# Six instead of seven key tiles added on VectorE, and layer-norm statistics by bn_stats, in a two-layer graph attention kernel

## The chip, the cores and the metric

The kernel runs on one core of a Trainium2 chip. The metric is the device time of one execution in microseconds, lower is better. Before the change it is 4522.25 us, the median of three runs (4520.34 to 4522.34).

## What is computed

There are 8 entries of 2048 nodes with 256 features, and one adjacency matrix of 2048 x 2048 for all. Each entry goes through two attention layers, each with a residual and a layer norm behind it:

```python
def _layernorm(x, axis=-1, eps=1e-5):
    m = jnp.mean(x, axis=axis, keepdims=True)
    v = jnp.var(x, axis=axis, keepdims=True)
    return (x - m) / jnp.sqrt(v + eps)

# layer 0, 8 heads of 32 features
x_proj = jnp.einsum('bnd,hdf->bhnf', x, W)
e = leaky_relu(e_src[..., :, None] + e_dst[..., None, :], 0.2)
e = e + (softplus(beta_tilde) * jnp.log(prior + 1e-6))[:, None, :, :]     # prior = adj
attn = softmax(where(adj > 0, e, neg_inf), axis=-1)
h = jnp.einsum('bhij,bhjf->bhif', attn, x_proj)      # ... reshaped to (B, N, D)
x = _layernorm(x + h @ W_out.T)

# layer 1, one head of 256 features
e = leaky_relu(jnp.einsum('bnd,bmd->bnm', x @ W1, x @ W2), 0.2)
attention = softmax(where(adj > 0, e, -1e12), axis=-1)
x = _layernorm(x + relu(jnp.einsum('bnm,bmd->bnd', attention, x @ W3)))
```

The softmax of layer 0 needs, for each query and head, the sum over 2048 keys of the unnormalised weights, the denominator. The layer norm needs a mean and a variance of each row of 256.

## The kernel before

Layer 0 goes over 4 head pairs x 16 key tiles = 64 steps per entry. A step makes one product `s` of 128 keys x 2048 queries per head on VectorE, and TensorE multiplies `s` by the values (`val`) and by the denominators' weights (`den`):

```python
SUMMED = (1, 3, 5, 7, 9, 11, 13)
...
mt = self.mts[jt] if first else load_mt(jt)
s = []
for a in range(HP):                                            # HP = 2 heads
    h = hp * HP + a
    sa = wide_tile("s", "s", 4)
    nc.vector.scalar_tensor_tensor(sa, self.cs[a], self.re[:, 0, jt, h:h + 1], mt, ALU.max, ALU.mult)
    s.append(sa)
...
summed = self.b > 0 and jt in SUMMED
if self.b > 0 and jt - 1 in SUMMED[1:]:
    for d, sa, h in zip(self.sums, self.last, heads):
        nc.vector.scalar_tensor_tensor(d, sa, e[:, jt - 1, h:h + 1], d, ALU.mult, ALU.add)   # line 311
self.last = s
self.products(self.val, [v[:, jt, ts(h, DH)] for h in heads], s, jt == 0, jt == NT - 1)
if self.b > 0 and jt == SUMMED[0]:
    self.sums = [wide_tile("d", "d", 2) for _ in heads]
    for d, sa, h in zip(self.sums, s, heads):
        nc.scalar.activation(d, sa, AF.Copy, scale=e[:, jt, h:h + 1])
if not summed:
    self.products(self.den, [e[:, jt, h:h + 1].to_broadcast([P, DH]) for h in heads], s, jt == 0,
                  self.b == 0 and jt == NT - 1)
if self.b > 0 and jt == NT - 1:
    self.products(self.den, [ones] * HP, self.sums, False, True)
```

For a key tile in `SUMMED` the denominator's share is not multiplied on TensorE: the tile is scaled and added into `d`, one tile per head, and `d` is multiplied by ones once at the end of the head pair. The first of them is scaled by ScalarE, the rest are added by VectorE one step later. Entry 0 has no such sums.

`products` issues eight matmuls, four of 32 columns beside one another in the array (two heads, two halves of the queries); each fp32 matmul shows as two records in the trace.

The residual and the norm, used in `output` on each of 16 row tiles after the W_out product `y` (which lies in one of three PSUM slots), and at the end of each of the 16 layer-1 steps of an entry:

```python
def add_norm(z, a, b):
    f = small.tile([P, 6], F32, name="f", bufs=3)
    total, shift, squares, log, factor, bias = (f[:, k:k + 1] for k in range(6))
    nc.vector.tensor_tensor_reduce(z, a, b, 1.0, 0.0, ALU.add, ALU.add, total)
    nc.scalar.mul(shift, total, -1.0 / D)
    sq = small.tile([P, D], BF16, name="sq", bufs=1)
    nc.scalar.activation(sq, z, AF.Square, bias=shift, accum_out=squares)
    nc.scalar.activation(log, squares, AF.Ln, bias=eps_ln, scale=1.0 / D)
    nc.scalar.activation(factor, log, AF.Exp, scale=-0.5)
    nc.scalar.activation(bias, factor, AF.Identity, scale=shift)
    nc.scalar.activation(z, z, AF.Identity, bias=bias, scale=factor)
```

Layer 1 of one entry and layer 0 of the next run woven together. The order of TensorE is that of the program; the other engines are ordered by the scheduler:

```python
if dot is not None:
    dot.step()                                     # the last layer-1 step of the entry before
layer_0(2)                                         # two steps ahead of the W_out products
for k, _ in enumerate(gat.output()):               # 16 W_out products with their norm
    if k % 8 == 7:
        layer_0(1)
for k, _ in enumerate(gat.turn()):                 # 16 transposes and h3 products
    if k % 2 == 1:
        layer_0(1)
dot = Dot(gat)
dot.step(lambda k: layer_0((2, 1, 1)[k]))
for i in range(NT - 2):
    dot.step(lambda k: layer_0((0, 2 - (i % 2 == 1), 2 - (i % 14 == 13))[k]))
```

The stretch from the W_out products to the end of `turn` is called the seam here, the layer-1 steps after it the long stage. A seam and a long stage make a cycle; there are seven cycles with layer-0 work of a next entry, and an eighth without.

Of the kernel before, what the change touches and what calls it, by code (L numbers as in the profile page):

```python
# [9 lines left out]
F32 = mybir.dt.float32  # L10
BF16 = mybir.dt.bfloat16
I32 = mybir.dt.int32
AF = mybir.ActivationFunctionType
ALU = mybir.AluOpType
# [4 lines left out]
P = 128  # L19
# [8 lines left out]
def kernel(  # L28
# [26 lines left out]
    nc = tc.nc  # L55
    B, N, D = x.shape
# [6 lines left out]
    HP = 2  # L63
    NP = H // HP
    IG = BK // P
    SUMMED = (1, 3, 5, 7, 9, 11, 13)

    const = ctx.enter_context(tc.tile_pool(name="const", bufs=1))
    dram = ctx.enter_context(tc.tile_pool(name="dram", bufs=1, space=DRAM))
# [3 lines left out]
    small = ctx.enter_context(tc.tile_pool(name="small", bufs=3))  # L73
# [3 lines left out]
    def mm_tile(name):  # L77
        return ps.tile([P, BK], F32, tag="mm", name=name)

    def wide_tile(name, tag, bufs, dtype=F32):  # L80
        return wide.tile([P, N], dtype, tag=tag, name=name, bufs=bufs)
# [12 lines left out]
    eps_ln = const.tile([P, 1], F32)  # L94
# [92 lines left out]
        nc.vector.tensor_scalar(pen, a, 0.0, NO_EDGE, ALU.is_le, ALU.mult)  # L187
        nc.sync.dma_start(pen_d[ts(it, P), :], pen)

    def add_norm(z, a, b):  # L190

        f = small.tile([P, 6], F32, name="f", bufs=3)
        total, shift, squares, log, factor, bias = (f[:, k:k + 1] for k in range(6))
        nc.vector.tensor_tensor_reduce(z, a, b, 1.0, 0.0, ALU.add, ALU.add, total)  # L194
        nc.scalar.mul(shift, total, -1.0 / D)
        sq = small.tile([P, D], BF16, name="sq", bufs=1)
        nc.scalar.activation(sq, z, AF.Square, bias=shift, accum_out=squares)  # L197
        nc.scalar.activation(log, squares, AF.Ln, bias=eps_ln, scale=1.0 / D)
        nc.scalar.activation(factor, log, AF.Exp, scale=-0.5)
        nc.scalar.activation(bias, factor, AF.Identity, scale=shift)  # L200
        nc.scalar.activation(z, z, AF.Identity, bias=bias, scale=factor)  # L201

    def row_tile(name, bufs=4):
        return small.tile([P, D], F32, tag="row", name=name, bufs=bufs)


    class Gat:
# [80 lines left out]
        def step(self, count=1):  # L288

            for _ in range(count):  # L290
                hp, jt = next(self.units)
                if jt == 0:
                    self.cs = [self.query_rows(hp * HP + a) for a in range(HP)]
                    self.val = pacc.tile([P, HALF], F32, tag="val", name="val")
                    self.den = pacc.tile([P, HALF], F32, tag="den", name="den")
                first = self.b == 0 and hp == 0
                while first and len(self.mts) < min(jt + 2, NT):
                    self.mts.append(make_mt(len(self.mts)))
                mt = self.mts[jt] if first else load_mt(jt)
                s = []  # L300
                for a in range(HP):
# [4 lines that stand above are left out]
                v, e = self.v, self.re[:, 1]  # L306
                heads = [hp * HP + a for a in range(HP)]
# [3 lines that stand above are left out]
                        nc.vector.scalar_tensor_tensor(d, sa, e[:, jt - 1, h:h + 1], d, ALU.mult, ALU.add)  # L311
# [11 lines that stand above are left out]
                if jt == NT - 1:  # L323
                    self.finish(hp)
# [33 lines left out]
        def output(self):  # L358


            b = self.b
            self.h3 = h3 = whole.tile([P, NT, D], F32, tag="h3", name="h3")
            xb = x[b].rearrange("(t p) d -> p t d", p=P)
            for g in range(NB):
                nc.sync.dma_start(h3[:, ts(g, IG), :], xb[:, ts(g, IG), :])
            for it in range(NT):
                y = mm_tile("y")
                for g, ht in enumerate(self.hts):
                    nc.tensor.matmul(y[:, 0:D], ht[:, ts(it, P)], wot[:, g, :], start=(g == 0), stop=(g == 1))  # L369
                z = h3[:, it, :]  # L370
                add_norm(z, y[:, 0:D], z)
                nc.sync.dma_start(x1_d[b, ts(it, P), :], z)
                yield

# [19 lines left out]
    class Dot:  # L394
# [33 lines left out]
        def step(self, fill=lambda k: None):  # L428


            it, (p, den) = self.at, self.ahead
            self.at += 1
            fill(0)

            def turned(g):
                t = mm_tile("pt")
                for k in range(IG):
                    nc.tensor.transpose(t[:, ts(k, P)], p[:, ts(g * IG + k, P)], ident)  # L438
                pt = chunk.tile([P, BK], F32, tag="pt", name="pts", bufs=2)
                nc.scalar.copy(pt, t)  # L440
                return pt

            pt = turned(0)
            if it + 1 < NT:
                if (it + 1) % IG == 0:
                    self.queries((it + 1) // IG)
                self.scores(it + 1)
            fill(1)
            acc = pacc.tile([P, D], F32, tag="acc", name="acc")
            for g in range(NB):  # L450
                now, pt = pt, turned(g + 1) if g + 1 < NB else None
                for k in range(IG):
                    j = g * IG + k
                    nc.tensor.matmul(acc, now[:, ts(k, P)], self.h3[:, j, :], start=(j == 0), stop=(j == NT - 1))  # L454
            fill(2)
            rec = small.tile([P, 1], F32, name="rec1", bufs=2)
            nc.vector.reciprocal(rec, den)
            xr = row_tile("x1r")
            nc.sync.dma_start(xr, x1_d[self.b, ts(it, P), :])
            z = row_tile("z")  # L460
            nc.scalar.activation(z, acc, AF.Relu, scale=rec)  # L461
            add_norm(z, z, xr)
            nc.sync.dma_start(out[self.b, ts(it, P), :], z)


# [70 lines left out]
```

## Time and profile before

| | before |
|---|---|
| time, median of 3 runs | 4522.25 us |
| span of the profiled execution | 4520.6 us |
| first W_out product (end of entry 0's layer 0) | 579.4 us |
| one cycle of an entry, from W_out product to W_out product | 510.6 to 518.2 us |
| last cycle, without layer-0 work | 328.3 us |
| granted TensorE clock, mean | 0.980 |

In the profile a group of instructions has one row: line, engine, operation, output and inputs by their names in the program, shapes and count, then the busy time and the mean duration of one, then the idle time of the engine just before them and the engine that ended it. A row of waits names who waited, for whom, how long in total, how often, and the longest. Durations of instructions that follow one another on an engine overlap a little, so the price of one in a queue is read from start to start.

### The profile page before, as it was taken

The page shows a single profiled execution, that of the slowest core. Times are in us where ns is not written, and L with a number is a line of the kernel's source. Part 1 is how long each engine was busy: PE and PEld are TensorE (multiplying, and loading weights), DVE is VectorE, ACT ScalarE, POOL GpSimd, SP SyncE. Part 2 cuts the span into 40 slices and gives each one's busy share as a digit, 9 for nine tenths or more (in the row PEclk, how much of TensorE's full clock was granted, in tenths as well). Part 3 has the DMA queues.
Part 4 walks back from the last instruction along what each step waited for, and adds up shares of the span by engine and source line. Part 5 has one row for each costly group of instructions (what it writes and reads, how often), then busy time and mean ns, then how long its engine had stood idle before and what let it go on. Part 6 is the DMA issues. An engine that isn't in the chain of part 4 may idle for free. (4 is left out here: it accounts for less than half of the span.)

```text
span 4520.6 us, 60051 instructions
## 1 busy us (share of the span) xinstructions
PE 4247.3 (94%) x24476; PEld 2206.4 (49%) x24476; DVE 3651.3 (81%) x2397; ACT 1930.6 (43%) x4251; POOL 4.5 (0%) x14
## 2 busy tenths in 40 slices
PE   6888889999999989999999999999899999999899
PEld 4433334445454544455444554455454554455566
DVE  5787798888989988898998988898988989898111
ACT  6622244345343454344433453344443453443555
POOL 0000000000000000000000000000000000000000
PEclk9999999999999999999999999999999999999999
DMA  7788865556555465556554565555555565554211
GB/s 218 260 297 320 313 207 181 182 184 220 179 178 178 171 217 179 184 187 207 194 178 169 182 218 184 178 187 195 195 175 181 185 222 178 182 177 141 68 49 40
DMA packets 252773, 851.97 MB, mean 188 GB/s; under 512 B 33616, under 2 KB 152400, under 8 KB 174928
## 3 DMA queue, kind: packets, MB, share of 16 engines
q1 hardware_dynamic: 252496, 848.13, 54.1%
q8 instruction: 192, 3.15, 0.3%
q14 instruction: 85, 0.70, 0.0%
HBM read 772.15 MB, written 75.37 MB: 187 GB/s over the span
## 5 line engine op out<-in xcount | busy, mean ns | idle before, releaser
L304 DVE SCALAR_TENSOR_TENSOR s<-c,re,mt 128x2048 f32<-128x2048 f32 x1024 | 2352.4, 2348 | 179.7 <-PE den L329 70.9
L329 PE MATMUL val<-s,v 128*32 128x512 f32 x8192 | 1054.8, 612 | 128.8 <-DVE s L304 118.9
L454 PE MATMUL acc<-h,pts 128*128 128x256 f32 x4096 | 953.6, 381 | 22.0 <-ACT pts L440 22.0
L419 PE MATMUL e<-x1t,h 128*128 128x512 f32 x2048 | 904.1, 594 | 0.1
L454 PEld LDWEIGHTS acc<-h,pts 128*128 128x128 f32 x4096 | 748.0, 190 | 119.3 <-ACT pts L440 30.8
L311 DVE SCALAR_TENSOR_TENSOR d<-s,re,d 128x2048 f32<-128x2048 f32 x336 | 782.7, 2347 | 0.0
L329 PE MATMUL den<-s,re 128*32 128x512 f32 x5056 | 642.9, 599 | 0.0
L329 PEld LDWEIGHTS val<-s,v 128*32 128x32 f32 x8192 | 245.3, 111 | 758.4 <-issue 494.6
L419 PEld LDWEIGHTS e<-x1t,h 128*128 128x128 f32 x2048 | 379.4, 190 | 450.3 <-issue 423.7
L421 ACT ACTIVATE p<-e 128x512 f32<-128x512 f32 x512 | 303.6, 596 | 479.7 <-PE e L419 479.6
L440 ACT COPY pts<-pt 128x512 f32<-128x512 f32 x512 | 295.2, 583 | 497.2 <-PE pt L438 496.8
L424 DVE CUSTOM_DVE_ANT_0 p<-p,pen 128x2048 f32<-128x2048 f32 x128 | 293.1, 2290 | 234.4 <-ACT p L421 234.4
L425 ACT ACTIVATE p<-p,neg 128x2048 f32<-128x2048 f32 x128 | 256.7, 2006 | 291.3 <-DVE neg L424 290.8
L329 PEld LDWEIGHTS den<-s,re 128*32 128x32 f32 x5056 | 177.5, 112 | 388.1 <-issue 386.7
L438 PEld LDWEIGHTS pt<-ident,p 128*128 128x128 f32 x2048 | 238.0, 141 | 224.8 <-issue 155.1
L438 PE MATMUL pt<-ident,p 128*128 128x128 f32 x2048 | 318.7, 279 | 5.9 <-ACT p L425 5.1
L461 ACT ACTIVATE z<-acc,rec 128x256 f32<-128x256 f32 x128 | 60.8, 475 | 399.0 <-PE acc L454 245.2
L194 DVE CUSTOM_DVE_ANT_0 z<-z,x1r 128x256 f32<-128x256 f32 x128 | 54.3, 424 | 181.8 <-ACT z L461 181.8
L369 PE MATMUL y<-wot,ht 128*128 128x256 f32 x512 | 140.4, 428 | 55.4 <-DVE ht L356 35.7
L369 PEld LDWEIGHTS y<-wot,ht 128*128 128x128 f32 x512 | 104.4, 212 | 97.0 <-DVE ht L356 38.5
L317 ACT ACTIVATE d<-s,re 128x2048 f32<-128x2048 f32 x56 | 112.2, 2003 | 64.3 <-DVE ht L356 45.1
L388 PE MATMUL h3p<-w3s,x1t 128*128 128x256 f32 x512 | 132.6, 384 | 4.6 <-ACT x1t L384 4.6
(83 smaller groups left out, 2118.1 us busy)
## 6 DMA issues: line engine op xcount, KB each, us to landing
mt<-mt_d SPq DMA_DIRECT2D x496, 1024.0 KB, 4.8
c<-c_d SPq DMA_DIRECT2D x64, 1024.0 KB, 5.6
pen<-pen_d SPq DMA_DIRECT2D x128, 512.0 KB, 3.3
xr<-in_x_dram SPq DMA_DIRECT2D x16, 1024.0 KB, 8.0
adj_t<-in_adj_dram SPq DMA_DIRECT2D x16, 1024.0 KB, 7.6
mt_d<-mt SPq DMA_DIRECT2D x16, 1024.0 KB, 5.5
adj_r<-in_adj_dram SPq DMA_DIRECT2D x16, 1024.0 KB, 8.4
rb<-rec_d SPq DMA_DIRECT2D x64, 256.0 KB, 4.1
```

The lines of the kernel that those rows point to most:

```text
L304: nc.vector.scalar_tensor_tensor(sa, self.cs[a], self.re[:, 0, jt, h:h + 1], mt, ALU.max, ALU.mult)
L311: nc.vector.scalar_tensor_tensor(d, sa, e[:, jt - 1, h:h + 1], d, ALU.mult, ALU.add)
L329: nc.tensor.matmul(dst[ts(q, DH), ts(c, BK)], weights[q % 2], s[q % 2][:, ds(q // 2 * HALF + c * BK, BK)], start=start, stop=stop)
L369: nc.tensor.matmul(y[:, 0:D], ht[:, ts(it, P)], wot[:, g, :], start=(g == 0), stop=(g == 1))
L388: nc.tensor.matmul(t[:, 0:D], x1t[:, kc, ts(it - 1, P)], w3s[:, kc, :], start=(kc == 0), stop=(kc == KC - 1))
L419: nc.tensor.matmul(t, self.h1[:, kc, ts(it % IG, P)], self.x1t[:, kc, ts(c, BK)], start=(kc == 0), stop=(kc == KC - 1))
L421: nc.scalar.activation(p[:, ts(c, BK)], t, AF.Prelu, alpha=ALPHA)
L424: nc.vector.tensor_tensor_reduce(p, p, pen, -1.0, FMAX, ALU.add, ALU.min, neg)
L425: nc.scalar.activation(p, p, AF.Exp, bias=neg, scale=-1.0, accum_out=den)
L438: nc.tensor.transpose(t[:, ts(k, P)], p[:, ts(g * IG + k, P)], ident)
L440: nc.scalar.copy(pt, t)
L454: nc.tensor.matmul(acc, now[:, ts(k, P)], self.h3[:, j, :], start=(j == 0), stop=(j == NT - 1))
```

## The change

The sums on VectorE take six key tiles, 1, 3, 6, 8, 11 and 13, instead of seven; the seventh tile's denominator goes back to TensorE. The norm takes mean and variance from VectorE's bn_stats and bn_aggr instead of a row sum fused into the add and a Square pass on ScalarE. The aim is to move work between the three engines: a pass over 2048 elements from VectorE to TensorE, and a pass over 256 elements from ScalarE to VectorE. The two layer-0 steps ahead of the W_out products are the same in both kernels.

```diff
-    SUMMED = (1, 3, 5, 7, 9, 11, 13)
+    SUMMED = (1, 3, 6, 8, 11, 13)
...
-    def add_norm(z, a, b):
-
-        f = small.tile([P, 6], F32, name="f", bufs=3)
-        total, shift, squares, log, factor, bias = (f[:, k:k + 1] for k in range(6))
-        nc.vector.tensor_tensor_reduce(z, a, b, 1.0, 0.0, ALU.add, ALU.add, total)
-        nc.scalar.mul(shift, total, -1.0 / D)
-        sq = small.tile([P, D], BF16, name="sq", bufs=1)
-        nc.scalar.activation(sq, z, AF.Square, bias=shift, accum_out=squares)
-        nc.scalar.activation(log, squares, AF.Ln, bias=eps_ln, scale=1.0 / D)
-        nc.scalar.activation(factor, log, AF.Exp, scale=-0.5)
-        nc.scalar.activation(bias, factor, AF.Identity, scale=shift)
-        nc.scalar.activation(z, z, AF.Identity, bias=bias, scale=factor)
+    def layer_norm(z):
+
+        st = small.tile([P, nc.vector.BN_STATS_DIM], F32, name="st", bufs=2)
+        nc.vector.bn_stats(st, z)
+        mv = small.tile([P, nc.vector.BN_AGGR_DIM], F32, name="mv", bufs=3)
+        nc.vector.bn_aggr(mv, st)
+        f = small.tile([P, 4], F32, name="f", bufs=3)
+        nc.scalar.activation(f[:, 0:1], mv[:, 1:2], AF.Ln, bias=eps_ln)
+        nc.scalar.activation(f[:, 1:2], f[:, 0:1], AF.Exp, scale=-0.5)
+        nc.scalar.mul(f[:, 2:3], mv[:, 0:1], -1.0)
+        nc.scalar.activation(f[:, 3:4], f[:, 1:2], AF.Identity, scale=f[:, 2:3])
+        nc.scalar.activation(z, z, AF.Identity, bias=f[:, 3:4], scale=f[:, 1:2])
...
-                add_norm(z, y[:, 0:D], z)
+                nc.vector.tensor_add(z, y[:, 0:D], z)
+                layer_norm(z)
...
-            add_norm(z, z, xr)
+            nc.vector.tensor_add(z, z, xr)
+            layer_norm(z)
```

## The prediction

> **What bounds the kernel now.** I read the busy shares first, then TensorE's idle time stage by stage, then who ends it, and last the price of each operation concerned.
>
> The first part of the page, and from its list of groups the two sides of the trade (each row: busy time, mean ns of one, idle before them and its releaser):
>
> ```profile
> PE 4247.3 (94%) x24476; PEld 2206.4 (49%) x24476; DVE 3651.3 (81%) x2397; ACT 1930.6 (43%) x4251; POOL 4.5 (0%) x14
> ...
> L311 DVE SCALAR_TENSOR_TENSOR d<-s,re,d 128x2048 f32<-128x2048 f32 x336 | 782.7, 2347 | 0.0
> L329 PE MATMUL den<-s,re 128*32 128x512 f32 x5056 | 642.9, 599 | 0.0
> ```
>
> TensorE is busy 94% of the span and VectorE 81%, so averages do not settle it. Windows on the third seam and what follows it do. The columns are stage, length, busy time of TensorE, its weight loads, VectorE, ScalarE, GpSimd, clock, DMA share, GB/s. The first window is the W_out products, the second the turn and h3 products, the third the layer-1 steps of one entry with 52 layer-0 steps of the next between them:
>
> ```profile
> 1615.60:1644.80 29.20, 22.52 (x116) 14.03 (x112) 22.44 (x37) 23.52 (x92) 0.00 (x0) 0.94 0.78 254
> 1644.80:1698.10 53.30, 48.76 (x301) 22.58 (x297) 53.30 (x28) 17.10 (x56) 0.00 (x0) 0.97 0.47 164
> 1698.10:2131.90 433.80, 425.63 (x2473) 216.17 (x2471) 378.81 (x232) 178.21 (x314) 0.00 (x0) 1.00 0.54 187
> ```
>
> In the long stage TensorE is idle for 433.8 - 425.6 = 8.2 us and VectorE for 55.0 us: TensorE is the bound there. In the turn stage VectorE has no idle time at all (53.30 of 53.30), and TensorE loses 4.5 us. In the W_out stage TensorE loses 6.7 us. The waits of TensorE in the two seam stages together, and then in the long stage (total, times, longest):
>
> ```profile
> PE y L369 <- DVE ht L356: 4.6, 1, 4.6
> PE val L329 <- DVE s L304: 3.1, 3, 1.2
> PE y L369 <- DVE f L194: 2.1, 2, 1.1
> ```
>
> ```profile
> PE val L329 <- DVE s L304: 5.0, 1, 5.0
> PE acc L454 <- ACT pts L440: 3.1, 5, 0.7
> ```
>
> So a cycle of one entry, 516.3 us here (2131.9 - 1615.6), holds about 19 us in which TensorE does nothing, and all but 4.6 us of it ends with VectorE. The 5.0 us wait follows a VectorE queue that was held by the load of mt and then by a penalty pass of 2.29 us put ahead of the product; I find it once in each of the two cycles I looked at.
>
> **What the Trainium skill says.** "Perfetto Trace Analysis", § Identifying the Most-Contended Engine: matmul busy time is a poor measure of the distance to roofline. The trace agrees in that weight loads fill only 49%; but here the question is only whether more matmuls lengthen the queue, and idle time of 8 us in 434 answers that. The same page, § Optimizing Scalar/DVE Operations, says that every VectorE instruction has a fixed cost, some 60 ns on SBUF, so that few large operations beat many small ones. The trace agrees in kind: a reciprocal of one element per partition takes 160 ns. "VectorE: DVE Perf Modes", § The perf-mode tier table: an fp32 tensor_tensor of 2048 elements runs at the 1x rate in 2293 ns; the one in the trace (line 356) takes 2290 ns. "TensorE: Matmul & The Clock Gate", Part 3 (Packing small matmuls): products on different tiles of the array run side by side. The trace agrees: sixteen den records of 599 ns would need 9.6 us one by one and take 1.72 us. No page gives a time for bn_stats or bn_aggr.
>
> **The change part by part.** The two steps ahead of the W_out products are already in the kernel before; only two things differ.
>
> *(1) Six tiles instead of seven.* The first tile of each sum is a ScalarE copy in both, so VectorE adds fall from 6 to 5 per head. They concern entries 1 to 7, four head pairs, two heads: 7 x 4 x 2 = 56 adds fewer, 56 x 2.347 = -131 us of VectorE. In their place 7 x 4 = 28 more sets of den products. TensorE's timeline shows their price (start, length, what):
>
> ```profile
> 1597.04 1.90 PE L329 MATMUL den<-s,re 128*32 128x512 f32 x16
> 1598.76 1.90 PE L329 MATMUL den<-d,ones 128*32 128x512 f32 x16
> 1600.59 1.09 PE L438 MATMUL pt<-ident,p 128*128 128x128 f32 x8
> ```
>
> From start to start a set of sixteen records costs 1.72 us. 28 x 1.72 = +48.2 us of TensorE, 6.9 us in each of seven cycles: one set in the seam (head pair 0) and three, 5.2 us, in the long stage.
>
> *(2) Statistics of the layer norm.* It runs 256 times. Per tile VectorE loses the fused add-and-sum and its accumulator read and gains a plain add, a bn_stats over 256 elements and a bn_aggr; ScalarE loses the Square pass and its accumulator read:
>
> ```profile
> L197 ACT ACTIVATE sq<-h,f 128x256 bf16<-128x256 f32 x128 | 63.7, 497 | 0.8
> ...
> L194 DVE CUSTOM_DVE_ANT_0 h<-y,h 128x256 f32<-128x256 f32 x128 | 52.8, 422 | 64.5 <-ACT h L201 30.0 <-PE y L369 20.5 <-ACT f L195 8.4
> ...
> L118 DVE TENSOR_TENSOR wa<-wp,a_bc 128x256 f32<-128x256 f32 x4 | 1.5, 422 | 4.1 <-DMA a_bc<-in_L_gnn_a_dst_dram 3.1 <-DMA a_bc<-in_L_gnn_a_src_dram 1.0
> L119 DVE TENSOR_REDUCE wp<-wa 128x8 f32<-128x256 f32 x4 | 1.5, 412 | 0.0
> ```
>
> The add should cost 422 ns (line 118). bn_stats reads 256 elements, so I take the 412 ns of line 119's reduce for it; bn_aggr has six numbers to read, for which I take the 160 ns of a one-element operation. These two are estimates. VectorE: 422 + 412 + 160 - 424 - 84 = +486 ns per tile, x 256 = +124 us. ScalarE: -(503 + 187) ns per tile, about -177 us, with the other five passes of the same kind as before.
>
> VectorE's busy time thus hardly moves in sum (-131 + 124 = -7 us), ScalarE's falls by 177, TensorE's rises by 48.
>
> **Where it lies on the path.** *Long stage*, per cycle: TensorE +5.2 us. VectorE there: three pairs of adds fewer, -14.1 us, sixteen norms more, 16 x 0.486 = +7.8 us, so -6.3 us, on an engine that already has 55 us free. Of the waits only the 5.0 us one could shrink by that, and it hangs on a transfer and on the order of the queue. I book +5.2.
> *Seam*, per cycle: VectorE is the bound there. It gets one pair of adds less in the turn stage (tiles 3, 6, 8 are added after steps 4, 7, 9, where before 3, 5, 7, 9 were added after 4, 6, 8, 10): -4.7 us. It gets 16 norms, +7.8 us: +3.1 us. Against that, VectorE sat idle for 6.8 us in the W_out stage, 4.3 of them for ScalarE's norm chain through the three f buffers (waits on h of line 201 and sq), which become shorter and no longer hold VectorE. TensorE's own +1.7 us fits beside. I book +1 us, between -2 and +4.
> Sum per cycle about +6.2, x 7 = +43 us.
> *Last seam* (4192 to 4248): no layer-0 work, and ScalarE paces the W_out products: two tiles every 3.17 us, 1.59 us each. With about 0.69 us less on ScalarE the pace becomes TensorE's own, about 1.0 us (in the third seam four tiles in a row take 3.98 us): up to 16 x 0.59 = 9 us, of which I count 6. The last 16 layer-1 steps are TensorE's and unchanged, as are the first 579 us, for entry 0 sums nothing. The closing chain of the last tile trades a Square pass for bn_stats: nothing.
> 4522.3 + 43 - 6 = 4559; I shade to 4557.
>
> **Rivals.** *A: VectorE was the true bound and TensorE's work is hidden.* For it: the turn stage, and that nearly all of TensorE's waits end with VectorE. Against it: those waits are 8 us in 434, and the sum of VectorE's work does not fall. If the 5 us wait vanished in all seven cycles, 35 us come back and the time is about 4522. *B: small operations choke the seam.* bn_stats and bn_aggr follow the add one upon another, each between 2.3 us products in an in-order queue; if bn_aggr takes 0.4 us, or the PSUM slots of y come free later, the seam grows by 4 to 6 us instead of 1, and the time is 4580 to 4595. *C: ScalarE's relief counts in every seam.* In the seams with layer-0 work VectorE would have to stop being full; it does not, so this is worth no more than the +1 assumes; were it 4 us a seam, the time is 4535.
>
> **Range and chances.** The TensorE term is safe to a microsecond or two; the seam is +-3 us a cycle and the 5 us wait can go either way, together some +-25 us. Range 4528 to 4582. Two per cent is 90 us: reaching 4432 needs all of TensorE's waits in the cycles to go and more, 4613 needs each seam to grow by over 10 us. Faster 0.01, same 0.96, slower 0.03.
>
> **What would show it.** den<-s,re should count 5056 + 448 = 5504 records, the adds of line 311's kind 280, TensorE busy some 4295 us, VectorE about 3645, ScalarE about 1755. The long stage should last some 439 us with TensorE's idle time there still near 8; seams about 83 us; the last seam about 49. It is wrong if VectorE waits in the long stage go away with the lighter queue (faster), or if y waits for VectorE's statistics for over 5 us a seam (slower).

## The result and the profile after

The changed kernel takes 4483.57 us (median of 4 runs, 4482.89 to 4488.59), the kernel before 4522.3 us beside it: ratio 0.9916, 95% interval 0.9899 to 0.9934. That is 0.84% faster. The prediction had 4557 us, slower by 0.8%, and a range that began at 4528.

The first part of the page of the changed kernel, and from its list of groups the two sides of the trade:

```profile
PE 4269.1 (95%) x24924; PEld 2218.7 (50%) x24924; DVE 3649.6 (81%) x2597; ACT 1769.7 (39%) x3739; POOL 4.5 (0%) x14
...
L329 PE MATMUL den<-s,re 128*32 128x512 f32 x5504 | 699.6, 596 | 0.0
L311 DVE SCALAR_TENSOR_TENSOR d<-s,re,d 128x2048 f32<-128x2048 f32 x280 | 651.8, 2347 | 0.0
```

Counts are as worked out (5504 den records, 280 adds), and so is VectorE's sum: 3649.6 us against the 3645 forecast. TensorE, though, is busy for only 22 us more, not 48. Windows on the same seam and long stage as before (columns as there):

```profile
1602.20:1629.50 27.30, 22.72 (x116) 15.26 (x112) 23.82 (x49) 17.47 (x65) 0.00 (x0) 0.87 0.75 254
1629.50:1684.80 55.30, 50.58 (x317) 22.91 (x314) 55.30 (x30) 15.85 (x50) 0.00 (x0) 1.00 0.48 164
1684.80:2114.00 429.20, 427.18 (x2521) 217.11 (x2519) 372.70 (x242) 165.31 (x282) 0.00 (x0) 1.00 0.54 189
```

The seam is 82.6 us where it was 82.5. The long stage fell from 433.8 to 429.2 us, although it holds 48 more den records, at a granted clock of 1.00 before and after. TensorE's waits in the seam, and then in the long stage, of the changed kernel:

```profile
PE y L369 <- DVE ht L356: 4.6, 1, 4.6
PE val L329 <- DVE s L304: 3.7, 5, 1.2
PE h3p L389 <- ACT x1t L385: 1.0, 2, 0.8
```

```profile
PE acc L455 <- ACT pts L441: 1.9, 3, 0.8
```

The 5.0 us wait of val for s is gone from the long stage. This holds in every cycle, and seven times -4.9 us (434.2 to 429.3, the means of five cycles), -2.9 us in the last cycle and -0.6 before the first seam make -37.8 of the -38.8 us between the two spans.

Where the wait had been, VectorE's queue differs. In the rows, mt is the step's tile made from the adjacency matrix, and ht the output of the heads, multiplied by the reciprocals rb of its denominators. The penalty pass (p<-p,pen) adds the penalty for missing edges to a row tile of layer 1's scores and takes the extreme value that their softmax needs. First VectorE, then TensorE, in the kernel before (start, length, what, and in brackets the idle time ahead of it and its releaser):

```profile
1869.16 2.29 DVE L356 TENSOR_TENSOR ht<-ht,rb 128x2048 f32<-128x2048 f32 x1 [3.21 <-DMA rb<-rec_d]
1874.29 2.35 DVE L304 SCALAR_TENSOR_TENSOR s<-c,re,mt 128x2048 f32<-128x2048 f32 x1 [2.84 <-PE e L419]
1879.04 2.29 DVE L424 CUSTOM_DVE_ANT_0 p<-p,pen 128x2048 f32<-128x2048 f32 x1 [2.40 <-ACT p L421]
...
1881.26 6.87 DVE L304 SCALAR_TENSOR_TENSOR s<-c,re,mt 128x2048 f32<-128x2048 f32 x3
```

```profile
1870.68 7.03 PE L419 MATMUL e<-x1t,h 128*128 128x512 f32 x16
1877.64 1.04 PE L329 MATMUL val<-s,v 128*32 128x512 f32 x2
1883.66 2.50 PE L329 MATMUL val<-s,v 128*32 128x512 f32 x11 [4.97 <-DVE s L304]
...
1888.92 0.66 PE L438 MATMUL pt<-ident,p 128*128 128x128 f32 x4
```

And in the changed kernel, in the same step:

```profile
1856.26 4.62 DVE L304 SCALAR_TENSOR_TENSOR s<-c,re,mt 128x2048 f32<-128x2048 f32 x2 [2.15 <-DMA mt<-mt_d]
1860.79 2.29 DVE L356 TENSOR_TENSOR ht<-ht,rb 128x2048 f32<-128x2048 f32 x1
1865.87 2.29 DVE L425 CUSTOM_DVE_ANT_0 p<-p,pen 128x2048 f32<-128x2048 f32 x1 [2.80 <-ACT p L422]
...
1868.09 9.14 DVE L304 SCALAR_TENSOR_TENSOR s<-c,re,mt 128x2048 f32<-128x2048 f32 x4
```

```profile
1858.17 7.03 PE L420 MATMUL e<-x1t,h 128*128 128x512 f32 x16
1865.13 1.92 PE L329 MATMUL val<-s,v 128*32 128x512 f32 x16
1866.87 1.90 PE L329 MATMUL den<-s,re 128*32 128x512 f32 x16
1868.70 0.66 PE L439 MATMUL pt<-ident,p 128*128 128x128 f32 x4
```

A step needs two products s, one per head. Before, the penalty pass of the next layer-1 row stood between the two: head 0's s, then the penalty pass, which waits for ScalarE's last p, which waits for the e products that TensorE runs just ahead of this val; then head 1's s. TensorE thus waited for a product that VectorE did not start until TensorE's own e products had gone through ScalarE and a penalty pass. In the changed kernel both products stand ahead of it. Counted in VectorE's order over the whole program, the kernel before has 21 such splits, three per entry, at the steps (hp, jt) = (0, 15), (2, 2) and (3, 15), both counted from 0 as in the code. The changed one has 7, all at (0, 15). The step shown is (2, 2).

But the kernel before also had the load of mt later: it was issued behind three rb loads and an output store, as the queue that loads mt shows:

```profile
1862.24 2.88 SPq L354 DMA_DIRECT2D rb<-rec_d  x3
1868.36 0.36 SPq L463 DMA_DIRECT2D out_dram<-z  x1
1868.76 0.93 SPq L180 DMA_DIRECT2D mt<-mt_d  x2
```

(The row of head 0's s puts its 2.84 us down to PE e; a cycle earlier the same row puts 3.99 us down to the load of mt.) So there were four candidates: the place of the penalty pass (P), the late load (Q), VectorE's lighter load (V) and the norm (N). The expectations call the wait the jam.

### The profile page after: what moved, and what is told of

It reads as the page before. It is cut to its first block, busy times and chain, and to the rows that moved or that the text cites. A ratio compares the mean times of both kernels' runs of the same rounds, so it can differ in the third digit from the quotient of the medians.

```text
span 4481.8 us, 60564 instructions
## 1 busy us (share of the span) xinstructions
PE 4269.1 (95%) x24924; PEld 2218.7 (50%) x24924; DVE 3649.6 (81%) x2597; ACT 1769.7 (39%) x3739; POOL 4.5 (0%) x14
## 4 chain that ended last, share of the span: by engine, by line
PE 65%; DVE 15%; issue 8%; ACT 4%; DMA 3%; SPq 0%; DVEq 0%; POOL 0%; POOLq 0%
PE acc L455 17%; PE e L420 15%; PE val L329 13%; DVE s L304 10%; PE den L329 9%; PE pt L439 4%; DVE d L311 3%; PE h1p L409 2%; DMA mt<-mt_d 1%; PE proj L248 1%; PE y L369 1%; ACT p L426 1%; PE h3p L389 1%; ACT h L201 1%; DMA x_d<-h 1%
## 5 line engine op out<-in xcount | busy, mean ns | idle before, releaser
L329 PE MATMUL den<-s,re 128*32 128x512 f32 x5504 | 699.6, 596 | 0.0
L311 DVE SCALAR_TENSOR_TENSOR d<-s,re,d 128x2048 f32<-128x2048 f32 x280 | 651.8, 2347 | 0.0
L329 PEld LDWEIGHTS den<-s,re 128*32 128x32 f32 x5504 | 191.7, 111 | 418.2 <-issue 418.2
L463 DVE TENSOR_TENSOR z<-z,x1r 128x256 f32<-128x256 f32 x128 | 54.2, 424 | 203.3 <-ACT z L462 191.4
L197 ACT ACTIVATE f<-mv,eps_ln 128x1 f32<-128x1 f32 x256 | 74.3, 290 | 203.6 <-DVE mv L195 202.5
```

The source lines that it names most:

```text
L329: nc.tensor.matmul(dst[ts(q, DH), ts(c, BK)], weights[q % 2], s[q % 2][:, ds(q // 2 * HALF + c * BK, BK)], start=start, stop=stop)
```

## The experiments

All times are medians of runs beside the kernel before; "seam" and "long" are means of the second to sixth cycle, in us. Line numbers in the rows differ by one or two between kernels.

| kernel | time | ratio to before (95%) | seam | long | last cycle to TensorE's end |
|---|---|---|---|---|---|
| before | 4519 to 4523 | | 82.6 | 434.2 | 322.2 |
| changed | 4483.6 | 0.9916 (0.9899, 0.9934) | 82.6 | 429.3 | 319.3 |
| E1 six sums, old norm | 4466.2 | 0.9883 (0.9868, 0.9898) | 80.7 | 428.0 | 324.0 |
| E2 seven sums, new norm | 4546.2 | 1.0057 (1.0042, 1.0072) | 85.0 | 435.3 | 319.9 |
| E3 rb loads elsewhere | 4497.8 | 0.9949 (0.9933, 0.9966) | 86.1 | 426.4 | 320.7 |
| E4 output store elsewhere | 4533.5 | 1.0033 (1.0020, 1.0046) | 83.7 | 435.0 | 323.7 |
| E5 one step's s first | 4478.9 | 0.9906 (0.9891, 0.9920) | 82.6 | 427.9 | 322.3 |
| E6 six sums, split put back | 4513.4 | 0.9982 (0.9975, 0.9989) | 80.7 | 434.9 | 324.3 |
| E7 five sums | 4495.8 | 0.9944 (0.9929, 0.9959) | 79.0 | 433.5 | 325.7 |
| E8 six sums, all s first | 4518.4 | 0.9990 (0.9981, 0.9999) | 86.4 | 429.5 | 326.1 |
| E9 six sums, norms mixed | 4474.7 | 0.9899 (0.9883, 0.9916) | 81.3 | 429.3 | 322.8 |
| E10 three steps ahead | 4489.3 | 0.9933 (0.9918, 0.9948) | 77.1 | 434.6 | 326.3 |
| E11 three steps' s first | 4492.3 | 0.9940 (0.9926, 0.9955) | 84.9 | 428.0 | 324.1 |

### E1 and E2: each half of the change alone

E1, on the kernel before:

```diff
-    SUMMED = (1, 3, 5, 7, 9, 11, 13)
+    SUMMED = (1, 3, 6, 8, 11, 13)
```

> Kernel before with six sums (1, 3, 6, 8, 11, 13) and the old norm (row sum fused into the add, Square on ScalarE). Theory Q (order of the DMA queue): with six sums the load of mt stands ahead of two of the rb loads and of the output store in the one DMA queue, so the jam in the middle of each long stage (7.8 to 8.8 us from block start to block start) goes away; den costs +5.2 us: long stage about 431 us, time 4480 to 4495. Rival N (it is the norm that removed the jam): the jam stays, long stage about 439 us, time 4545 to 4560. Rival V (VectorE's relief by 14 us of adds per long stage removed it): as Q.

E2, on the changed kernel:

```diff
-    SUMMED = (1, 3, 6, 8, 11, 13)
+    SUMMED = (1, 3, 5, 7, 9, 11, 13)
```

> The changed kernel with seven sums (1, 3, 5, ..., 13) and the new norm (bn_stats). Theory Q: mt stands behind all rb loads and the output store again, as in the kernel before; the jam stays, long stage 431 to 435 us, the seam 2 to 4 us longer than before for VectorE's extra work: time 4520 to 4545. Rival N: no jam, long stage about 424 us, time 4450 to 4470. Rival V: jam stays or grows, as Q or slower.

The sums carry the whole gain and more: E1 is at 4466 us, below what I expected, with no long wait of val in the long stage; E2 is slower than the kernel before, 1 us above the range expected under Q, and has the same 4.97 us wait. N falls: the norm costs 17 us with six sums (4466.2 to 4483.6) and 25 with seven. Of the four combinations E1 is the fastest.

### E3 and E4: the queue of transfers

E3, on the kernel before:

```diff
-                nc.sync.dma_start(rb[ts(a, DH), :]...
+                nc.gpsimd.dma_start(rb[ts(a, DH), :]...
```

> Kernel before, all work the same, only the loads of rb (reciprocals of the denominators) issued from GpSimd's queue instead of the queue that loads mt. Theory Q: mt is no longer held, the jam goes away with VectorE's work unchanged: long stage about 426 us (434.4 - 8.3), time 4460 to 4475. Rival V: VectorE's work is the same, so the jam stays: 4515 to 4530.

E4, on the kernel before:

```diff
-            nc.sync.dma_start(out[self.b, ts(it, P), :], z)
+            nc.scalar.dma_start(out[self.b, ts(it, P), :], z)
```

> Kernel before, only the store of the output rows issued from ScalarE instead of the queue that loads mt; mt still stands behind three rb loads but no longer behind the store, whose norm ended at 1350.9 us; the last rb load was issued at 1347.1. Theory Q: mt comes some 4 us earlier, the jam shrinks by 3 to 5 us a cycle: time 4487 to 4502. Rival V: 4515 to 4530.

E3 loses the wait, 7.8 us a cycle in the long stage, with all of VectorE's work in place, so V falls. (Its time falls by less and misses Q's range: in the seam y now waits 9.2 us for ht, and the first part took 590 us, 10 longer.) For Q it looked right, but E4 contradicts it. VectorE and then TensorE in E4:

```profile
1867.99 2.29 DVE L356 TENSOR_TENSOR ht<-ht,rb 128x2048 f32<-128x2048 f32 x1 [3.31 <-DMA rb<-rec_d]
1870.35 2.35 DVE L304 SCALAR_TENSOR_TENSOR s<-c,re,mt 128x2048 f32<-128x2048 f32 x1
1877.77 2.29 DVE L424 CUSTOM_DVE_ANT_0 p<-p,pen 128x2048 f32<-128x2048 f32 x1 [5.07 <-ACT p L421]
...
1879.99 6.87 DVE L304 SCALAR_TENSOR_TENSOR s<-c,re,mt 128x2048 f32<-128x2048 f32 x3
```

```profile
1876.38 1.05 PE L329 MATMUL val<-s,v 128*32 128x512 f32 x2
1882.39 2.78 PE L329 MATMUL val<-s,v 128*32 128x512 f32 x11 [4.97 <-DVE s L304]
```

Here mt is in time: head 0's product follows ht at once. Then VectorE sits idle for 5.07 us ahead of the penalty pass, with head 1's product of the same step, which uses the same mt, behind it. TensorE's wait is the same 4.97 us as before, so the late load did not make it. (E4's 4533.5 us lies above both ranges expected; seam and long stage are 1.1 and 0.8 us longer than before.) What E3 had changed as well was VectorE's order: there three products stand ahead of ht, and no penalty pass splits this step:

```profile
1867.29 6.88 DVE L304 SCALAR_TENSOR_TENSOR s<-c,re,mt 128x2048 f32<-128x2048 f32 x3 [2.65 <-PE den L329]
1874.08 2.28 DVE L356 TENSOR_TENSOR ht<-ht,rb 128x2048 f32<-128x2048 f32 x1
```

### E5 and E6: the order alone, both ways

E5, on the kernel before, raises the priority of one step's two products:

```diff
+                    with (tc.high_priority() if self.b > 0 and hp == 2 and jt == 2 else ExitStack()):
-                    nc.vector.scalar_tensor_tensor(sa, self.cs[a], ...)
+                        nc.vector.scalar_tensor_tensor(sa, self.cs[a], ...)
```

> Kernel before, seven sums and old norm, all work the same; only the two products of the third step of head pair 2 (one step in 64 per entry) get a higher priority, so that VectorE's queue has both of them ahead of the penalty pass instead of one ahead and one behind. Theory P (the place of the penalty pass in VectorE's queue, between the products of two heads of one step, made the jam): the jam goes away but for a wait of at most 1.5 us for the load of mt; long stage 426.5 to 428.5 us, time 4462 to 4482. Rival Q (the late load of mt): mt is as late as before, the jam stays, 4515 to 4530.

E6, on E1, puts one edge of order per entry, from the last penalty pass to head 1's s, which adds no work and no wait for data:

```diff
-                    nc.vector.scalar_tensor_tensor(sa, self.cs[a], ...)
+                    ins = nc.vector.scalar_tensor_tensor(sa, self.cs[a], ...)
+                    if self.b > 0 and hp == 2 and jt == 2 and a == 1:
+                        tc.add_manual_dep(ins.ins, pens[-1].ins.name, ..., reason='order')
...
-            nc.vector.tensor_tensor_reduce(p, p, pen, ...)
+            pens.append(nc.vector.tensor_tensor_reduce(p, p, pen, ...))
```

> Kernel of six sums with the old norm (4466 us), plus one order edge per entry that puts the second product of that same step behind the penalty pass; mt is loaded in time and no work is added. Theory P: the jam comes back, 7 to 9 us in each of seven long stages, long stage about 436 us, time 4515 to 4530. Rival Q: mt is in time, so no jam: 4460 to 4475. Rival V (six sums free VectorE): VectorE's idle time hides it, 4460 to 4475.

VectorE in E5, and TensorE there:

```profile
1855.60 2.29 DVE L357 TENSOR_TENSOR ht<-ht,rb 128x2048 f32<-128x2048 f32 x1 [3.06 <-DMA rb<-rec_d]
1860.69 4.61 DVE L305 SCALAR_TENSOR_TENSOR s<-c,re,mt 128x2048 f32<-128x2048 f32 x2 [2.80 <-DMA mt<-mt_d]
1865.64 2.29 DVE L425 CUSTOM_DVE_ANT_0 p<-p,pen 128x2048 f32<-128x2048 f32 x1 [0.34 <-ACT p L422]
```

```profile
1857.28 7.03 PE L420 MATMUL e<-x1t,h 128*128 128x512 f32 x16
1864.24 2.60 PE L330 MATMUL val<-s,v 128*32 128x512 f32 x13
...
1868.92 0.66 PE L439 MATMUL pt<-ident,p 128*128 128x128 f32 x4
```

The load of mt is as late as before (2.80 us of waiting for it), and yet val runs on: only the order was changed, and 4522.95 became 4478.9. The long stage lost 6.3 us, and 7 x 6.3 = 44 us is the whole difference. E6 is the reverse. VectorE and then TensorE in E6:

```profile
1870.19 2.35 DVE L304 SCALAR_TENSOR_TENSOR s<-c,re,mt 128x2048 f32<-128x2048 f32 x1 [2.65 <-PE den L331]
1872.46 2.28 DVE L358 TENSOR_TENSOR ht<-ht,rb 128x2048 f32<-128x2048 f32 x1
1879.98 2.29 DVE L426 CUSTOM_DVE_ANT_0 p<-p,pen 128x2048 f32<-128x2048 f32 x1 [5.23 <-ACT p L423]
...
1882.20 4.61 DVE L304 SCALAR_TENSOR_TENSOR s<-c,re,mt 128x2048 f32<-128x2048 f32 x2
```

```profile
1879.24 1.05 PE L331 MATMUL val<-s,v 128*32 128x512 f32 x2
1884.60 2.78 PE L331 MATMUL val<-s,v 128*32 128x512 f32 x11 [4.31 <-DVE s L304]
...
1889.74 0.66 PE L440 MATMUL pt<-ident,p 128*128 128x128 f32 x4
```

The lightly loaded kernel of six sums, whose long stage has over 60 us of VectorE idle, takes 6.9 us more per long stage (434.9 for 428.0) and 47 us in all, which is 2 us short of the range expected. P is shown in both directions; Q and V fall. The wait shows in all seven long stages of the kernel before (4.97 us each) and of E6 (4.31 each), and in none of E5 and of the changed kernel.

### E7: is a set of den products still worth 1.72 us?

```diff
-    SUMMED = (1, 3, 6, 8, 11, 13)
+    SUMMED = (1, 4, 7, 10, 13)
```

> Old norm, five sums (1, 4, 7, 10, 13): one more set of den products per head pair on TensorE than with six, 56 adds fewer on VectorE. If TensorE is the bound of the long stage and a set costs 1.72 us there: long stage 428.0 + 5.2 = 433.2 us; the seam the same or up to 2 us longer: time 4500 to 4518. If VectorE were the bound after all (rival V): faster than 4466.

Windows on the third long stage of E1, and then of E7:

```profile
1675.90:2103.80 427.90, 426.94 (x2521) 217.09 (x2519) 364.54 (x226) 178.37 (x314) 0.00 (x0) 1.00 0.54 190
```

```profile
1686.80:2120.30 433.50, 431.94 (x2569) 218.66 (x2567) 349.06 (x218) 178.66 (x314) 0.00 (x0) 1.00 0.53 187
```

From six to five the long stage grows by 5.5 us, TensorE's busy time by 5.0: three sets of 1.72 us are 5.2. The time itself, 4496, is a little below the 4500 to 4518 expected, since the seam became 1.7 us shorter and not longer. The added set of den products falls into the W_out stage there (29.3 us in E1, 31.4 in E7), but TensorE's idle time in the turn stage falls from 3.5 to 0.8 us with one pair of adds less on VectorE. So TensorE was the bound of the long stage, and the term of 5.2 us was right where nothing else is in the way.

From seven to six without the split (E5 to E1) the long stage grows by only 0.1 us (427.9 to 428.0). Counting TensorE's time from the start of each product to the start of the next, means of five cycles, shows where the 5.2 us went. The step with the late mt took 1.2 us longer in E5 (4.68 us in the cycle shown, 1864.24 to 1868.92, where two sets in the changed kernel take 3.57). Two other steps took 0.7 us longer. The transposes of layer 1's weights, with the products that read them, took 3.2 us longer (146.8 and 143.6), of which the view of waits shows 2.4 as waits for ScalarE's copies (3.3 to 0.9). Together this is 5.0 us that seven sums cost elsewhere in the stage. Why these copies come later with seven sums was not tested. Against E3, where mt is in time, six sums cost 1.6 us (426.4 to 428.0).

### E8 and E11: more of the same order

E8 gives the higher priority (200) to all products s of entries 1 to 7, with six sums:

> Six sums, old norm, all products s of entries 1 to 7 with a higher priority in the scheduler, so that no penalty pass is left between two heads. Theory P: the seventh-stage jams are gone already with six sums; the split that is left, one per entry in the seam's first penalty pass, costs at most 1 us: time 4455 to 4470. If priority delays the penalty passes and with them the transposed weights, slower: up to 4500.

E11 is E5 with two more steps, the last of head pairs 1 and 4 (hp 0 and 3 in the code):

```diff
-hp == 2 and jt == 2
+(hp, jt) in ((0, 15), (2, 2), (3, 15))
```

> Seven sums, old norm, with the higher priority also for steps 16 of head pairs 1 and 4, which had a penalty pass between two heads' products as well but showed no wait over 1 us on TensorE. Theory P, that such a split costs only where TensorE reaches the second product before VectorE does: no change from 4479, within 4470 to 4485. If every split costs: 4440 to 4460.

E8 has no split left and is 52 us slower than E1. A cycle takes 5.7 us more in the seam, where TensorE does nothing for 4.0 to 5.0 us between two y products (second to seventh cycle), besides the 4.6 us wait for ht that E1 has too, and 1.5 us more in the long stage. In E11 the long stage is as in E5 (428.0 and 427.9), but only the split of head pair 1 is gone: at (3, 15) the penalty pass still stands between the two products. That neither split costs shows in the steps themselves: (0, 15) and (3, 15) each take 5.29 us on TensorE, from their first product to the product after them, in every entry with sums of the kernel before, E5, E1, E7 and E11, whether they are split or not. The new order at the seam, though, makes y wait 3.1 us for the norm's row sum in E11, and the seams are 2.3 us longer. A split is harmful in one place of three; a priority meant to remove it can hurt elsewhere. Both missed what I expected: E8 lies 18 us above even the slower of its two cases, E11 7 us above its range. E7, with five sums, has no split at all without any change of priority.

### E9: where the new norm costs

The changed kernel with the old norm at the W_out products and the new one in the layer-1 steps:

> Six sums; the W_out products keep the old norm, the layer-1 steps take the new one (add, bn_stats, bn_aggr). If the new norm costs in the seam because VectorE is full there, the seam goes back to about 80.5 us (82.6 in the changed kernel) and the long stage stays at 429.3: time about 4475 (4466 + 7 x 1.3). If the new norm's cost sits in the layer-1 steps: seam 80.5 and long stage over 430, time over 4480. If it is in neither but in the queue order as a whole: anywhere else.

The seam comes back by 1.3 us (82.6 to 81.3), the long stage stays at 429.3, and the time is the 4475 expected. So of the norm's cost per cycle about 1.3 us lie in the seam, where VectorE is full, and 1.3 in the long stage. The remaining 0.6 us of the seam against E1 are two more long seams among the five: E9 has three of 81.9 us and two of 80.2, E1 one of 81.9 and four of 80.3. In the long stage the 1.3 us lie in the transposes of layer 1's weights and the products that read them (143.6 us from start to start in E1, 144.9 in the changed kernel). The new norm pays in the last cycle only, where no layer-0 work runs: 319.3 us for E1's 324.0.

### E10: a third step ahead of the W_out products

```diff
-        layer_0(2)
+        layer_0(3)
...
-            if k % 8 == 7:
+            if k == 11:
```

> Six sums, old norm, three steps of layer 0 ahead of the W_out products and one within them, where it was two and two: the third step's products of 3.4 us on TensorE could fill most of the 4.6 us wait of y for ht. VectorE's queue still has ht's product before that step's s, so the gain needs s to come early: if it does, 2 to 4 us a cycle, 4440 to 4455; if TensorE, in program order, waits for that s instead of for ht, nothing or slower, 4460 to 4485.

Seam and long stage together are 511.7 us for E1's 508.7: the step moved ahead and the 4.6 us wait for ht is gone, but TensorE waits 0.74 and 1.22 us for that step's s, and y then waits for the norm's row sum, 2.9 us at the longest. In the third W_out stage TensorE is idle for 5.4 us, where E1, ht's wait included, has 6.4. The time lands just above the range for "nothing or slower".

## Why the prediction was wrong

**What held.** The counts, VectorE's sum and the price of a set of den products (E7). The seam, booked at +1 us, did not move (82.6 and 82.6): -1.9 from the sums, +1.9 from the norm. The norm's price was near the estimate. Its rows in the changed kernel:

```profile
L193 DVE BATCH_NORM_STATS2 st<-z 128x6 f32<-128x256 f32 x128 | 54.6, 427 | 2.2
L463 DVE TENSOR_TENSOR z<-z,x1r 128x256 f32<-128x256 f32 x128 | 54.2, 424 | 203.3 <-ACT z L462 191.4 <-DMA rb<-rec_d 11.9
...
L371 DVE TENSOR_TENSOR h<-y,h 128x256 f32<-128x256 f32 x128 | 52.8, 413 | 25.7 <-PE y L369 25.6
L193 DVE BATCH_NORM_STATS2 st<-h 128x6 f32<-128x256 f32 x128 | 52.1, 422 | 0.8
...
L195 DVE BATCH_NORM_AGGREGATE mv<-st 128x2 f32<-128x6 f32 x256 | 45.4, 177 | 4.7 <-ACT f L199 0.8
```

bn_stats was put at 412 ns and takes 422 to 427, bn_aggr at 160 and takes 177; with the add at 413 to 424 that is +512 ns per tile where I had +486. Rival B, small operations that choke the seam, did not come.

**The step that failed** is the one on the long stage: "Of the waits only the 5.0 us one could shrink by that, and it hangs on a transfer and on the order of the queue. I book +5.2." The wait did not shrink, it vanished, because a different list of summed tiles led the scheduler to another order of VectorE's queue. I had seen the penalty pass ahead of the product, and left the wait in place as though the order were a property of the kernel that the change does not touch. It is decided anew when the program changes: 21 splits with seven sums, 7 with six, none with five (E7). The second term of that step failed with it: the +5.2 of the den products, held to be "safe to a microsecond or two", came to +0.1, since with six sums TensorE's other steps became 5.0 us shorter (E5 and E1). The terms of the long stage, per cycle, against the runs:

| | booked | shown by |
|---|---|---|
| 5 us wait | 0 | -6.3 (E5 against before) |
| one more set of den products per head pair, three in the stage | +5.2 | +0.1 net (E1 against E5), +1.6 (E1 against E3); +5.5 where nothing offsets it (E7 against E1) |
| norm in the layer-1 steps | 0 | +1.3 (E9 and the changed kernel against E1) |
| sum | +5.2 | -4.9 |

Over seven cycles this is 71 of the 73 us between forecast and result: 44 for the wait, 36 for the den products, less 9 for the norm.

**The size of the wait** was wrong too. The view of waits gives 4.97 us. But from its first product to the product after it the step takes 11.28 us in the kernel before (1877.64 to 1888.92) and 3.57 in the changed one, 7.7 us less; over the seven cycles the difference is 7.3 to 8.9. What the view does not show stands in the trace as busy time of val and den, which run on in fragments (val x2, val x11, den x1, val x3, den x15) long after the idle time ends. It is 3.1 us in the mean of five cycles; over seven cycles that is 22 us, most of the 26 by which TensorE's busy time stayed below the forecast growth of 48. Of all this E5 took away 6.3 us net, since the late mt still stretches its step by 1.2 us and a later step grew by 0.5. In E6 the step takes 10.50 us (1879.24 to 1889.74) where E1 has 3.57, and that is the whole 6.9 us of its longer stage, though the view shows a wait of 4.31.

**Rival A** named the outcome, "if the 5 us wait vanished in all seven cycles", and put it at 4522, but for VectorE's load, which E3, E5 and E6 exclude as the cause, and it kept the den term whole. Its "8 us in 434" is all of TensorE's idle time in the stage; the waits that end with VectorE are 5.0 of it. The last seam was booked at -6 us; the last cycle gained 2.9 (E1 to the changed kernel 4.7), since the W_out stage fell from 30.2 to 25.1 us and the turn stage after it grew from 25.3 to 27.5.

**What stays open:** why seven sums make the scheduler put the penalty pass between the two products and six do not. Of the two parts of the change the sums alone decide it (E1, E2), but E3 has seven sums and no split at that step, so other edits decide it too; by which rule the runs do not show.

## What to carry to other kernels

Where a scheduler sets the order of an engine's queue, a change to any instruction can move others: before booking a saved or added operation, look in the trace for waits on the bounding engine that come from the order of another engine's queue, and give them their own chance to vanish or appear, at more than their idle time. Here one product per entry behind a penalty pass cost as much (44 to 48 us) as the seventh tile's sums were meant to save on TensorE (48 us), with the engine concerned idle for over 50 us in the stage. Test such a wait by moving that one instruction (E5, E6), and measure the halves of a change apart: the faster half alone, E1 at 4466 us, beats both kernels.

## What was not expected of the hardware

A wait was worth more than the view of waits shows: 6.3 us came back where 4.97 were taken away (E5), and 6.9 were lost where 4.31 were put in (E6). bn_stats over 256 fp32 elements takes as long as an add of the same size (422 to 427 ns and 413 to 424). The first part of the program, the same work in all kernels, lasted between 576 and 590 us up to the first W_out product in the profiles, so that differences of a few microseconds in the whole time were read from the stages and not from the total.
